# Residual rows of a graph layer's second stage loaded through GpSimd's queue instead of ScalarE's

## The chip, the cores and the metric

One core of a Trainium2 chip. The metric is the device time of one execution in microseconds (us), median of several runs. For the kernel before it is 1530.25 us over 3 runs (1523.82 to 1533.23).

## What is computed

x has 8 batches of 4096 nodes with 256 features, adj is 4096 x 4096, W is 256 x 256; all are 32-bit floats.

```python
HW = einsum('bnf,fo->bno', x, W)
A = relu((adj + adj.T) * 0.5)
D = sum(A, axis=1)
d = where(D > 0, D ** -0.5, 0)
L = eye(4096) - d[:, None] * A * d[None, :]
x = layernorm(x + relu(einsum('nm,bmo->bno', L, HW)), axis=-1, eps=1e-5)
```

The inputs make adj sparse: node j is linked to node i with a probability that falls with both indices, and the diagonal is always set.

## The kernel before

The nodes are cut into 32 rows of 128 nodes. One "row" of x, of the product or of the output is a tile of 128 partitions (nodes) by 2048 values (8 batches of 256), 1 MB.

**First stage** (lines 398 to 670). adj is read in blocks of 512 x 512, transposed on TensorE and added to its mirror block on VectorE, put through relu on ScalarE and stored to a scratch array in HBM, `a_dram`. On the way sums over groups of 64 columns are kept (`part`). HW, scaled by d, is formed row by row and stored as `g_dram` (4096 rows of 8 KB). The product of the first row of 128 output nodes (`lead`) is made here too, because all of its blocks are needed.

**Second stage** (lines 768 to 1051). It makes the other 31 output rows, in blocks u of two rows (2u+1 and 2u+2; the last block, 15, has one), in the order 1 to 7, 0, 8 to 15. Since A is sparse, only some nodes m matter for a block. Lists made on the fly from `part` by VectorE and TensorE (functions `prepare` and `lists`, lines 937 to 985) pack up to 128 such nodes into one tile of the list. A tile of the list serves one or both of the rows and 64 or 128 nodes of each; its kind says which. For each tile:

- GpSimd gathers the tile's pieces of A (`ga`, line 814, 128 x 128 or 128 x 256) and the 128 rows of g (`g`, line 827, 1 MB) with two indirect DMAs, in `gather(n)`. The g tiles go into a ring of RING = 12 buffers, so gather n + 12 is emitted behind the products of tile n.
- TensorE multiplies them into four PSUM banks per row (line 1032). The first row of a block uses the banks b0, the second the banks b1. Two products that fill 64 partitions each run side by side.

A block has 9 to 26 tiles (table CAPS). When a row's last product is emitted, `finish(i)` follows (line 907): ScalarE evicts the four banks through relu with the scale -d into one buffer y (line 683; there is one such buffer), then VectorE adds y to the residual row of x, `xr` (line 693), takes mean and variance (lines 702 to 721) and normalises in place (line 726), and SyncE's queue stores the result (line 734). The last row, 31, is finished in four parts spread over ScalarE, VectorE and GpSimd (`finish_last`, line 858; the adds are at lines 874, 876, 882 and 887).

**Residual rows.** The tiles `xr` come from a pool of four 1 MB buffers (`blocks_pool`, line 395; shared with the first stage's blocks of adj). `residual(i, engine)` takes a buffer and issues one DMA on the queue of the engine given (line 677); in HBM the row is 1024 pieces of 1 KB. A buffer is free when the store of the row four places back has landed. Row 0's and the first block's are loaded by SyncE's queue ahead of the stage.

**Order of the work.** The program is written down in one order, and each engine takes its instructions in that order. `queue(engine)` pins an instruction behind the instruction last emitted on that engine, so that the scheduler does not move it. `after(n, fn, ...)` puts a piece of work off until n units of products are emitted; a unit is a tile's product for 64 nodes of one row. At the start of each block, `residuals` is put off by 10 units (4 for the last block):

```python
if new:
    after(6, prepare, u)
    if q > 0:
        after(10 if u != SEQ[-1] else 4, residuals, range(2 * u + 1, 2 * u + 1 + blocks(u)))
```

So the pair of residual loads of a block stands, in the emitted order, some five to ten tiles into the block. On ScalarE the neighbours of the pair are the evictions of the block before and those of the block itself; on GpSimd the neighbours are the gathers that run 12 tiles ahead of the products.

Of the kernel before, what the change touches and what calls it, by code (L numbers as in the profile page):

```python
# [59 lines left out]
def kernel(  # L60
# [25 lines left out]
    nc = tc.nc  # L86
# [88 lines left out]
    def blocks(u):  # L175

        return min(2, NB - 1 - 2 * u)
# [497 lines left out]
    def residual(i, engine):  # L675
        xr = blocks_pool.tile([P, B, F], F32, tag="adj", name=f"xr_{i}")
        engine.dma_start(xr, x[:, i * P : (i + 1) * P, :].rearrange("b p f -> p b f"))
        return xr
# [89 lines left out]
    with (  # L768
# [23 lines left out]
        def queue(engine):  # L792

            traced = reversed(nc.cur_bb.bb.instructions)
            return tc.issue_after(next(i for i in traced if i.engine == engines[engine]))
# [55 lines left out]
        xr = {i: residual(i, nc.sync) for i in (0, *range(2 * u + 1, 2 * u + 1 + blocks(u)))}  # L851
# [76 lines left out]

        def residuals(rows):
            for i in rows:  # L930
                with queue("act"):
                    xr[i] = residual(i, nc.scalar)


        ahead = {u: {k: SEQ[n + k] for k in (2, 3, 4) if n + k < NU} for n, u in enumerate(SEQ)}
# [58 lines left out]
        for q, (u, step) in enumerate(steps):  # L994
            new = q == 0 or steps[q - 1][0] != u
            last = q + 1 == len(steps) or steps[q + 1][0] != u
# [4 lines that stand above are left out]
                left = {}  # L1001
                for v, st in steps[q:]:
                    if v == u:
                        for k, t in st:
                            for b, _ in targets(u, k):
                                left[b] = left.get(b, 0) + 1
                begun = set()
                for b in range(blocks(u)):
                    py[2 * u + 1 + b] = []
# [103 lines left out]
```

## Time and profile before

| | us |
|---|---|
| median of 3 runs | 1530.25 |
| lowest and highest run | 1523.82, 1533.23 |
| profiled execution, span from the first to the last instruction | 1527.5 |
| PE busy | 1441.2 (94%) |
| DVE busy | 983.6 (64%) |
| POOL busy | 682.0 (45%) |
| ACT busy | 369.0 (24%) |
| L827, gathers of g, 268 | 294.9 busy |
| L814, gathers of A, 268 | 292.0 busy |
| L693, add of the residual, 31 | 71.1 busy |
| L677, residual loads on ScalarE's queue, 29 | 0.374 each to issue |

The page gives no time of the profiled execution other than its span; the runs' times are those of other executions.

PE is TensorE's matmul, PEld its weight loads, DVE is VectorE, ACT ScalarE, POOL GpSimd, SP SyncE. A number such as L827 is a line of the kernel. In the page's row pictures the span is cut into 40 slices of 38 us, and each digit is the busy share of a slice in tenths. The DMA row is the mean busy share of the core's 16 DMA engines. Matmuls are pipelined and their ends are modelled, so a full PE row alone does not say that PE is at its peak. In the lists of waits a line reads: engine, what waited, what it waited for, us in total, times, longest. Lines of the timeline read: start, length, engine, line, operation, out<-in, count, and in brackets the idle time before and what ended it.

### The profile page before, as it was taken

What the parts mean: (1) busy time and instruction counts of PE and PEld (TensorE: products, weight loads), DVE (VectorE), ACT (ScalarE), POOL (GpSimd) and SP (SyncE); (2) the same over time, 40 slices, a digit from 0 to 9 for tenths busy, and PEclk for the clock granted to TensorE, in tenths of its full rate; (3) what the DMA queues carried; (4) which work ended last, traced back from release to release, by engine and by line L of the source; (5) the groups of instructions that cost most, each with busy time, mean ns of one, the idle gap of its engine ahead of it and who ended that gap; (6) DMA issues with size and microseconds to landing.
All of it is one profiled execution on the core that took longest, in us unless ns stands there. A gap on an engine that the chain in (4) does not pass through costs nothing.

```text
span 1527.5 us, 19332 instructions
## 1 busy us (share of the span) xinstructions
PE 1441.2 (94%) x6440; PEld 763.6 (50%) x6440; DVE 983.6 (64%) x3015; ACT 369.0 (24%) x462; POOL 682.0 (45%) x1051
## 2 busy tenths in 40 slices
PE   5999999989989989999999999999999999999995
PEld 5778777767767754433343343333433433333331
DVE  4676578888646463055568769569137688898534
ACT  3655554535434450010100100100010010001111
POOL 3002010010303316666667666666556676656653
PEclk9999999989999999999999999999999999999998
DMA  9999999999879898999999999999979999999995
GB/s 340 365 366 401 393 379 365 359 369 354 344 248 367 332 390 354 401 395 418 361 393 372 402 409 365 393 403 389 384 278 406 346 394 403 405 393 366 379 405 195
DMA packets 216714, 564.50 MB, mean 370 GB/s; under 512 B 16550, under 2 KB 104918, under 8 KB 180134
## 3 DMA queue, kind: packets, MB, share of 16 engines
q0 software_dynamic: 54224, 304.94, 50.4%
q1 hardware_dynamic: 93472, 126.89, 23.8%
q10 hardware_dynamic: 68912, 131.37, 22.7%
q8 instruction: 54, 0.88, 0.2%
q14 instruction: 52, 0.43, 0.1%
HBM read 443.61 MB, written 136.34 MB: 380 GB/s over the span
## 4 chain that ended last, share of the span: by engine, by line
PE 68%; DMA 14%; DVE 9%; issue 5%; POOL 2%; ACT 2%; ACTq 0%; DVEq 0%; POOLq 0%
PE py L1032 49%; PE pg L532 8%; DMA g<-g_dram,gi 6%; PE lead L490 5%; DMA a_dram<-sym 5%; DVE sym L427 3%; PE xtr L521 2%; PE tr L423 2%; DVE part L432 2%; DMA xin<-in_x_dram 2%; DMA ga<-a_dram,ai 1%; ACT sym L431 1%; PE lists L356 1%; ACT xt L522 1%; POOL g L827 0%
## 5 line engine op out<-in xcount | busy, mean ns | idle before, releaser
L1032 PE MATMUL py<-g,ga 128*64 128x512 f32 (+1 forms) x2872 | 813.0, 600 | 18.4 <-DMA g<-g_dram,gi 8.0
L1032 PEld LDWEIGHTS py<-g,ga 128*64 128x64 f32 (+1 forms) x2872 | 293.1, 151 | 525.1 <-issue 493.1
L827 POOL DMA_INDIRECT g<-g_dram,gi x268 | 294.9, 1101 | 219.1 <-PE py L1032 79.1
L814 POOL DMA_INDIRECT ga<-a_dram,ai x268 | 292.0, 1090 | 109.5 <-issue 76.8
L683 ACT ACTIVATE y<-py,minus_r 128x512 f32<-128x512 f32 x120 | 79.9, 687 | 812.3 <-PE py L1032 659.8
L693 DVE TENSOR_TENSOR xr<-xr,y 128x2048 f32<-128x2048 f32 x31 | 71.1, 2294 | 269.1 <-ACT y L683 267.2
L532 PE MATMUL pg<-w_sb,xt 128*128 128x256 f32 x1024 | 232.0, 385 | 5.2 <-ACT xt L522 5.2
L427 DVE TENSOR_TENSOR sym<-tr,adj 128x512 f32<-128x512 f32 x256 | 162.7, 683 | 96.9 <-PE tr L423 80.2
L532 PEld LDWEIGHTS pg<-w_sb,xt 128*128 128x128 f32 x1024 | 195.6, 194 | 33.4 <-ACT xt L522 5.6
L432 DVE TENSOR_REDUCE part<-sym 128x32 f32<-128x2048 f32 x64 | 145.5, 2279 | 62.0 <-ACT sym L431 62.0
L423 PE MATMUL tr<-ident,adj 128*128 128x128 f32 x1024 | 138.4, 285 | 30.6 <-DVE sym L427 19.2
L431 ACT ACTIVATE sym<-sym 128x2048 f32<-128x2048 f32 x64 | 122.6, 1916 | 129.9 <-DVE sym L427 117.5
L452 POOL TENSOR_TENSOR r<-e,neg_half 128x4 f32<-128x4 f32 x8 | 8.3, 1039 | 317.9 <-DVE e L451 236.5
L423 PEld LDWEIGHTS tr<-ident,adj 128*128 128x128 f32 x1024 | 118.6, 146 | 60.4 <-DVE sym L427 32.1
L521 PE MATMUL xtr<-ident,xin 128*128 128x128 f32 x512 | 72.4, 288 | 18.0 <-DVE sym L427 16.5
L702 DVE BATCH_NORM_STATS2 stats<-xr 128x6 f32<-128x256 f32 x256 | 87.0, 413 | 1.1
L726 DVE TENSOR_SCALAR xr<-xr,mv,root 128x256 f32<-128x256 f32 x248 | 83.6, 409 | 0.1
L490 PE MATMUL lead<-gt,strip 128*128 128x512 f32 x176 | 83.0, 598 | 0.0
L522 ACT COPY xt<-xtr 128x512 f32<-128x512 f32 x128 | 68.1, 591 | 46.7 <-PE xtr L521 46.0
L542 ACT ACTIVATE gt<-pg,r 128x512 f32<-128x512 f32 x88 | 60.6, 688 | 74.8 <-PE pg L532 72.3
L1032 PE MATMUL py<-g_hub,ga 128*128 128x512 f32 x176 | 77.3, 592 | 0.0
L521 PEld LDWEIGHTS xtr<-ident,xin 128*128 128x128 f32 x512 | 59.0, 146 | 34.9 <-DVE sym L427 26.4
(142 smaller groups left out, 825.8 us busy)
## 6 DMA issues: line engine op xcount, KB each, us to landing
adj<-in_adj_dram SPq DMA_DIRECT2D x64, 1024.0 KB
a_dram<-sym ACTq DMA_DIRECT2D x64, 1024.0 KB
out_dram<-xr SPq DMA_DIRECT2D x31, 1024.0 KB
xr<-in_x_dram ACTq DMA_DIRECT2D x29, 1024.0 KB
xin<-in_x_dram SPq DMA_DIRECT2D x44, 512.0 KB
g_dram<-gt ACTq DMA_DIRECT2D x22, 1024.0 KB
xin<-in_x_dram POOLq DMA_DIRECT2D x20, 512.0 KB
g_dram<-held ACTq DMA_DIRECT2D x10, 1024.0 KB
```

The lines of the kernel that those rows point to most:

```text
L423: ins = nc.tensor.transpose(pt[:, c * P : (c + 1) * P], tji[:, c, a * P : (a + 1) * P], ident)
L427: nc.vector.tensor_add(sym[:, a, :], pt, tij[:, a, :])
L431: nc.scalar.activation(sym, sym, AF.Relu, scale=0.5)
L432: nc.vector.tensor_reduce(part[:, i * A : (i + 1) * A, j * S // Q : (j + 1) * S // Q], sym.rearrange("p a (c q) -> p a c q", q=Q), AX.X, A ...
L490: nc.tensor.matmul(lead[c], lhsT=strip, rhs=g[:, c * S : (c + 1) * S], start=not done, stop=len(done) == NB - 1, skip_group_check=True,)
L521: nc.tensor.transpose(pt[:, k, c, :], xin[b // H][:, b % H + k, c * P : (c + 1) * P], ident)
L532: ins = nc.tensor.matmul(pg[:, k * FO : (k + 1) * FO], lhsT=xt[:, b + k, c, :], rhs=w_sb[:, c, :], start=(c == 0), stop=(c == FC - 1),)
L702: nc.vector.bn_stats(stats[:, b, :], z[:, b, :])
L726: nc.vector.tensor_scalar(z[:, b, :], z[:, b, :], mv[:, b, 0:1], rstd[:, b : b + 1], ALU.subtract, ALU.mult,)
L814: nc.gpsimd.indirect_dma_start(out=at if both else at[:, :P], out_offset=None, in_=a_pairs if both else a_rows, in_offset=bass.IndirectOff ...
L827: nc.gpsimd.indirect_dma_start(out=gt, out_offset=None, in_=g_dram, in_offset=bass.IndirectOffsetOnAxis(ap=gi[:, t : t + 1], axis=0), boun ...
L1032: nc.tensor.matmul(py[2 * u + 1 + b][c][rows, :], lhsT=at[:, off + rows.start : off + rows.stop], rhs=gt[:, c * S : (c + 1) * S], start=ne ...
```

## The change

The function that issues the residual loads of a block names another engine, both for the DMA and for the pin on the order. The point in the emitted order stays.

```diff
         def residuals(rows):
             for i in rows:
-                with queue("act"):
-                    xr[i] = residual(i, nc.scalar)
+                with queue("pool"):
+                    xr[i] = residual(i, nc.gpsimd)
```

It concerns 29 loads of 1 MB: the rows of all blocks but the first. In the built program the instructions of TensorE, VectorE and SyncE keep their order. ScalarE loses 29 DMA issues. GpSimd gains 29, in pairs between two pairs of gathers, and the last one behind the last gather.

## Prediction

> **What bounds the kernel now.** I read the page first: busy shares, the 40 slices, the DMA queues.
>
> ```profile
> PE   5999999989989989999999999999999999999995
> POOL 3002010010303316666667666666556676656653
> DMA  9999999999879898999999999999979999999995
> ```
>
> From slice 16 on (about 600 us, the second stage) TensorE and the DMA engines are both full, and GpSimd is half busy. The stretch view puts numbers on it; its columns are the stretch, its length, busy time and instruction count of PE, PEld, DVE, ACT and POOL, then the granted clock, the DMA share and GB/s.
>
> ```profile
> 595.00:1150.00 555.00, 545.06 (x2109) 208.78 (x2109) 331.38 (x1267) 42.78 (x65) 364.86 (x339) 0.99 0.99 383
> 1150.00:1507.00 357.00, 348.71 (x1416) 131.21 (x1414) 265.22 (x1004) 37.82 (x56) 220.52 (x201) 0.99 1.00 386
> ```
>
> PE is busy for 893.8 of 912 us, so about 18 us is all that any better supply of data can give before the last products. The weight loads agree: they follow each other every 0.43 us, and the pauses over 1.1 us from start to start add up to 19 us, of which 5.6 lie between 1450 and 1500 us. The waits of GpSimd say what paces the gathers:
>
> ```profile
> POOL g L827 <- PE py L1032: 79.1, 56, 4.6
> POOL g L827 <- DMA g<-g_dram,gi: 48.6, 40, 2.8
> POOL ga L814 <- DMA g<-g_dram,gi: 24.9, 28, 2.0
> ```
>
> A gather waits for PE to free a ring buffer, or for an earlier gather's landing: in the built program every GpSimd DMA waits for the one eight places before it, so eight (four pairs ga and g) are in flight. The chain of waits shows that as steps of 13.0 to 14.2 us "DMA g" between 1436 and 1507 us. Matching each gather with the product that uses it, it is issued 13 to 40 us ahead of its use. The tightest are 12.6 us (near 921), 17.2 (1428) and 13.6 (1486).
>
> Now the residual loads. ScalarE issues them in pairs right after the last eviction of the block before, and VectorE's add needs them:
>
> ```profile
> 1441.98 3.93 ACTq L677 DMA_DIRECT2D xr<-in_x_dram  x2
> 1487.29 0.37 ACTq L677 DMA_DIRECT2D xr<-in_x_dram  x1
> ```
>
> ```profile
> 1430.32 2.29 DVE L693 TENSOR_TENSOR xr<-xr,y 128x2048 f32<-128x2048 f32 x1 [15.32 <-ACT y L683]
> 1442.64 2.29 DVE L693 TENSOR_TENSOR xr<-xr,y 128x2048 f32<-128x2048 f32 x1 [0.31 <-ACT y L683]
> 1476.44 2.29 DVE L693 TENSOR_TENSOR xr<-xr,y 128x2048 f32<-128x2048 f32 x1 [22.77 <-ACT y L683]
> 1489.28 2.29 DVE L693 TENSOR_TENSOR xr<-xr,y 128x2048 f32<-128x2048 f32 x1 [1.83 <-issue]
> ```
>
> The trace's packet records show the pair landing one behind the other, slowly: issued at 1442, landed at 1456.0 and 1488.5; issued at 678.5 and 679, landed at 693.3 and 718.6. The last one, issued at 1487.3, landed at 1510.9, and the first add that needs it starts at 1512.6.
>
> [...]a queue of 1 KB packets beside one of 4 to 8 KB packets gets a small share (26 to 75 GB/s against 250 to 365 for GpSimd's queue in the packet records).[...] The trace has 50 of 536 gathers above 1.5 us instead of 0.95 to 1.0, many of them starting within a microsecond of an L693 add.
>
> **The change part by part.** Removed from ScalarE's queue: 29 issues of 0.374 us. ScalarE idles 660 us before its evictions waiting for PE, so this gives nothing. Nor did the waits of these loads for their buffer: the longest hold it between 1345.9 and 1358.1, and its next eviction is at 1378.3.
>
> Added to GpSimd: 29 issues. No load of 1 MB in 1 KB runs is there on GpSimd, but its half is: xin took 758 ns for 512 runs, and 128 runs of 1 KB take 592 ns, so 1024 runs come to 758 + 512 x (758 - 592)/384 = 979 ns. Bounds: 758 ns, and twice 758 = 1516 ns. I take 1.0 us and 0.3 us between issues: 2 x 1.3 = 2.6 us per block of about 51 us. A pair of gathers needs 0.95 + 1.0 + 2 x 0.3 = 2.55 us, and pairs follow at 3.4 us (912/268), so some 15 pairs leave 12.7 us. Hidden; at 1516 ns it is 3.6 us, hidden too. If that cover were gone, 38 us would be at stake.
>
> Moved in time: a load now stands between the gathers of the same point in the emitted order. Counting GpSimd's DMAs, those points lie in the run before at 707, 772, 842, 904, 964, 1022, 1076, 1165, 1221, 1273, 1326, 1377, 1428 and 1475 us, and behind the very last gather (1497.7). That is 18 to 41 us later than now (10 for the last). In one queue with the gathers a load lands about 13 us after its issue, like a gather, and the second 3 us later. For the first load of each pair against its add:
> - 720 (add at 734.8), 785 (797.6), 1178 (1187), 1234 (1238.6), 1286 (1288): in time.
> - 855 (854.7), 1339 (1338.0): level.
> - 917 (911.4), 977 (970.8), 1035 (1029.6), 1390 (1384.1): 6 us late.
> - 1441 (1430.3), 1488 (1476.4): 11 to 12 us late.
>
> The second loads are all earlier than now or in time. What is late next where an add is 6 to 12 us late? Behind it on VectorE stand the statistics, the index lists and the add of the second row. The lists are first used by a gather 18 us or more after they are made (1439.2 to 1465.7, 1297.9 to 1318.4), so that holds. The second row's eviction needs the y buffer that the add frees: at 1441 + 2.3 = 1443.3 against 1439.4 now, but PE's next block writes the first row's banks for 3.4 us before it needs the second's; at 1490.3 against 1484.7 the last block uses the other banks alone. I cost it at nothing, up to 4 us. The wait for the buffer (the store four rows back) is over at least 10.8 us before each point (1261.6 against 1272.4 is the narrowest).
>
> Gathers behind a pair: 2.1 MB at 386 GB/s is 5.5 us of queue in front of them. But the same bytes no longer compete before that point, so the gathers before it run ahead; the count of bytes at the end of a block is equal. Nothing, up to 5.5 us where the lead is 12.6 to 17.2 us.
>
> DMA time itself. Three lines of the DMA view from 640 to 1500 us (packets, MB, share of 16 engines), and for GpSimd's loads the line of 347 to 531 us, where it moved xin in 1 KB runs:
>
> ```profile
> q0 software_dynamic: 45904, 269.62, 78.8%
> q10 hardware_dynamic: 30043, 30.30, 10.4%
> q1 hardware_dynamic: 29937, 30.19, 10.0%
> ```
>
> ```profile
> q0 software_dynamic: 3600, 11.73, 17.3%
> ```
>
> ScalarE's queue (q10) costs 0.104 x 860/30.30 = 2.95 us per MB, GpSimd's with 1 KB runs 0.173 x 184/11.73 = 2.71. A load gets 0.24 x 1.05 = 0.25 us cheaper, 29 of them 7.3 us. It counts only where PE then waits: the ring is nearly full (mostly 10 or 11 of 12 out) until 1310 us, so the 7 loads after it count, 7 x 0.25 = 1.8 us.
>
> The end. Between 1475 and 1507 us PE waits for gathers (2.9 and 1.8 us shown at 1500 and 1507). The last row's load, some 0.9 MB of which now moves before the last gather lands, then stands behind it: 0.9/0.386 = 2.4 us earlier. It lands about 3 us after that gather, and the products and evictions ahead of its add take 5.5 us. VectorE must do two rows of 11.0 us (1476.4 to 1487.5) after the late load: 1488 + 22.2 = 1510, against the 1513.4 at which the last row's add starts; a 4.2 us gain is just kept.
>
> Sum against the profiled execution: 1527.5 - 1.8 - 2.4 = 1523.3 us of span. The median of the runs, 1530.25, is 2.75 above that span (the page gives no other time of that execution), so 1526.0.
>
> **The rivals.** (1) Hidden anyway: PE paces everything, the freed DMA time is not used: 1530. For it: PE busy 98%; against it: the waits at the end.
> (2) Slower, gathers queue behind the bursts: where the lead is under 13 + 5.5 us a pair costs up to 5.5 us that PE doesn't regain. Places: 842, 904 to 921, 1428, 1475 to 1486, some three to four blocks, 16 to 22 us: 1547. It decides from three full losses on. For it: leads of 12.6 and 13.6; against it: bytes conserved.
> (3) Slower, late residuals hold VectorE: it is without a pause before its adds at 1238.6 and nearly so at 1288 and 1338. If loads land 10 us later than I say[...], each of four blocks loses about 8 us: 1562. It decides once a load is over 7 us late there, the lead of the lists' inputs (1233.8 against 1240.1).
> (4) All of the DMA saving counts, and the stores of rows 29 and 30 also slip behind the last gather (1 MB, 2.7 us): 1530.25 - 7.3 - 2.4 - 2.7 = 1518.
>
> **How the numbers follow.** Forecast 45%, (1) 23%, (2) 17%, (3) 6%, (4) 9%. A measurement here tells about 1% from no change (the three runs lie 0.6% apart). Faster by over 1% (under 1515): half of (4), 0.05. Slower by over 1% (over 1545.5): (3) and most of (2), 0.20. The rest, 0.75, is within 1%. The likeliest case alone runs from 1519 to 1532; the range that leaves out a tenth at either end is 1515 to 1549.
>
> **What would show it.** Right: L677 on GpSimd at about 1 us each; DMA share still 0.99 to 1.00; first loads landing 13 us after issue, adds at the four late points waiting for xr, the second adds earlier; PE's pauses after 1450 shorter; last gather landing a few us sooner. Wrong: new PE waits for g right behind the residual loads;[...] PE waiting for lists.

## The result, and the profile after

| | median us (lowest to highest) | runs |
|---|---|---|
| before | 1528.05 (1523.23 to 1533.23) | 17 |
| change | 1534.93 (1530.02 to 1538.35) | 17 |

The ratio is 1.0041 with the interval 1.0029 to 1.0053: the change is slower by 0.4%, some 6 us. The forecast was 1526.0, 4.2 us faster than the 1530.25 that three runs of the kernel before had given; over 17 runs that kernel's median is 2.2 us lower. The time lies in the range of 1515 to 1549, but it moved the other way. A repetition (e4 below) gave 1.0036.

The profiled execution of the change has a span of 1533.0 us. Its first add of the second stage starts at 601.5 us, against 595.7 before and 597.3 to 598.7 in four other profiles (e1 to e4 below, the change itself once more among them). Those 6 us are chance in a stage that the change does not touch. So times of the two profiles are compared here with 5.8 us taken off, and the net effect is read from the medians, not from the two spans.

The page of the kernel after, same rows as shown of before:

```profile
PE   5999998989989989999999999997999999999996
POOL 3002000010202225776667776776657687676663
DMA  9999999999879999999999999999979999999996
```

The stretches of the second stage (length; busy time and count of PE, PEld, DVE, ACT, POOL; granted clock, DMA share, GB/s):

```profile
595.00:1150.00 555.00, 540.26 (x2078) 207.21 (x2078) 325.32 (x1223) 43.09 (x64) 379.93 (x349) 0.99 0.98 381
1150.00:1507.00 357.00, 350.83 (x1438) 132.66 (x1436) 267.70 (x1011) 40.08 (x60) 248.96 (x224) 1.00 1.00 386
```

GpSimd's digits are up by one (once by two) in half of the slices: 15.1 + 28.4 = 43.5 us more in these stretches, of which the 29 issues are some 27. The DMA engines are about as full as they were (share 0.98 and 1.00, before 0.99 and 1.00). PE is busy for less of the first stretch (540.3 for 545.1 us) and for more of the second (350.8 for 348.7); with the stretches moved by 5.8 us its two numbers are the same. The groups of the residual tile (duration in ns: minimum, median, maximum; first and last start):

```profile
L693 DVE TENSOR_TENSOR xr<-xr,y x31: 2277/2292/2333, 601.5 to 1505.1; 128x2048 f32<-128x2048 f32 x31
L677 POOL DMA_DIRECT2D xr<-in_x_dram x29: 902/949/971, 710.9 to 1503.8; - x29
```

GpSimd's waits in the kernel after:

```profile
POOL g L827 <- PE py L1032: 62.9, 47, 5.9
POOL g L827 <- DMA g<-g_dram,gi: 19.9, 23, 1.3
POOL ga L814 <- DMA xr<-in_x_dram: 9.7, 6, 2.5
POOL g L827 <- DMA xr<-in_x_dram: 7.8, 5, 2.8
POOL xr L677 <- DMA g<-g_dram,gi: 2.2, 3, 1.0
```

A residual load issues in 0.95 us and hardly waits itself. Gathers now wait for residual loads among the eight places, 17.5 us in 11 waits, but they wait less for each other. What is new stands in PE's waits in the second stage. Before, PE waited mainly for gathered g, and once for VectorE's `pos_k`:

```profile
PE py L1032 <- DMA g<-g_dram,gi: 8.0, 5, 2.9
PE py L1032 <- issue: 6.9, 13, 0.8
PE py L1032 <- DVE pos_k L188: 2.2, 1, 2.2
```

After:

```profile
PE py L1032 <- DVE pos_k L188: 10.6, 2, 8.2
PE py L1032 <- issue: 4.1, 3, 1.9
PE py L1032 <- DVE half L720: 4.1, 1, 4.1
PE py L1032 <- DMA g<-g_dram,gi: 1.8, 3, 1.2
```

The longest of the waits with "issue" after, 1.92 us at 1359.5, ends 0.06 us behind an L188, at the end of the same block as the 2.2 us before (1349.4). So that one is not new.

Products do not read `pos_k`. It is the place on VectorE's queue behind which something came free, and the timeline of one block shows what. The first fence is the kernel before, the second the kernel after, at the end of the same block (lines picked from the timeline):

```profile
1029.62 2.29 DVE L693 TENSOR_TENSOR xr<-xr,y 128x2048 f32<-128x2048 f32 x1 [8.07 <-ACT y L683]
...
1032.94 0.96 PE L356 MATMUL lists<-val,hot 128*128 128x30 bf16 x32
...
1033.82 14.58 PE L1032 MATMUL py<-g,ga 128*64 128x512 f32 x57
...
1037.75 0.17 DVE L368 COPY low<-lists 128x15 f32<-128x15 f32 x1
...
1040.26 0.52 DVE L188 TENSOR_TENSOR pos_k<-incl_k,lists 128x352 f32<-128x352 f32 x1
```

```profile
1028.00 1.87 POOL L677 DMA_DIRECT2D xr<-in_x_dram  x2
...
1032.80 0.95 PE L356 MATMUL lists<-val,hot 128*128 128x30 bf16 x32
...
1033.68 8.80 PE L1032 MATMUL py<-g,ga 128*64 128x512 f32 x40
...
1039.49 2.29 DVE L693 TENSOR_TENSOR xr<-xr,y 128x2048 f32<-128x2048 f32 x1 [7.87 <-issue]
...
1041.88 2.42 ACT L683 ACTIVATE y<-py,minus_r 128x512 f32<-128x512 f32 x4 [13.02 <-DVE xr L693]
...
1047.86 0.17 DVE L368 COPY low<-lists 128x15 f32<-128x15 f32 x1
...
1050.14 0.52 DVE L188 TENSOR_TENSOR pos_k<-incl_k,lists 128x352 f32<-128x352 f32 x1
...
1050.72 5.72 PE L1032 MATMUL py<-g,ga 128*64 128x512 f32 x11 [8.24 <-DVE pos_k L188]
```

The two PSUM tiles of `lists(u)` carry the tag b0: they take two of the four banks that the first row of the next block accumulates in. They are free when VectorE has read them (L368 to L189; the first of the two behind L188), and VectorE does that behind the first row's add, its statistics and its inverse root, 8.1 us of work. Before, the add starts at 1029.6, L188 is done at 1040.8 and L189 at 1041.3, and PE does not stop. After, the load issued at 1028.0 lands 11.5 us later, the add starts at 1039.5, L188 at 1050.1, and PE, done with its 40 products at 1042.5, stands 8.24 us. The word "issue" in the bracket of L693 says only that the profile shows no releaser. That it is the load follows from the order: y had been evicted before, and in e3 below the same wait has the load named. The late add also keeps the second row's eviction (L683) 13.02 us from the one buffer y, but that eviction is over at 1044.3, more than 6 us before PE resumes.

That two banks are what PE waits for is read from the program and from the releaser that the trace names (PE resumes 0.06 us behind L188); no run put the lists into other banks.

In block 13 there is no L188 any more, and the last reading of the lists is L369:

```profile
1448.16 2.29 DVE L693 TENSOR_TENSOR xr<-xr,y 128x2048 f32<-128x2048 f32 x1 [22.15 <-issue]
...
1450.55 2.42 ACT L683 ACTIVATE y<-py,minus_r 128x512 f32<-128x512 f32 x4 [11.81 <-DVE xr L693]
...
1456.62 0.17 DVE L369 SCALAR_TENSOR_TENSOR low<-lists,low 128x9 f32<-128x9 f32 x1
...
1456.93 4.11 PE L1032 MATMUL py<-g,ga 128*64 128x512 f32 x8 [4.06 <-DVE half L720]
```

Here too the eviction of the second row stands for y, 11.81 us. But that eviction is over at 1453.0, and PE resumes only at 1456.93, 0.14 us behind the end of L369. The bracket names L720, which stands a few instructions ahead of L369 on VectorE; the second profile of the change names L369 itself at this place. So this pause too is put down to the lists' banks.

PE's pauses of 1 us or more add up to 19.3 us in the second stage of this execution, against 9.3 before.

### The profile page after: what moved, and what is told of

The parts are those of the page before. It is cut to its first block, busy times and chain, and to the rows that moved or that the text cites. A ratio compares the mean times of both kernels' runs of the same rounds, so it can differ in the third digit from the quotient of the medians.

```text
span 1533.0 us, 19317 instructions
## 1 busy us (share of the span) xinstructions
PE 1442.1 (94%) x6440; PEld 767.6 (50%) x6440; DVE 988.2 (64%) x3015; ACT 370.0 (24%) x462; POOL 721.8 (47%) x1080
## 2 busy tenths in 40 slices
DMA packets 194442, 564.50 MB, mean 368 GB/s; under 512 B 16550, under 2 KB 75222, under 8 KB 157862
## 4 chain that ended last, share of the span: by engine, by line
PE 51%; DMA 16%; issue 15%; DVE 11%; POOL 5%; ACT 1%; ACTq 0%; another core or an unknown queue 0%; POOLq 0%; DVEq 0%; SPq 0%
PE py L1032 34%; DMA g<-g_dram,gi 7%; PE pg L532 7%; PE lead L490 5%; DMA xr<-in_x_dram 3%; DVE sym L427 2%; DMA ga<-a_dram,ai 2%; PE tr L423 2%; PE xtr L521 2%; DVE part L432 2%; DMA a_dram<-sym 2%; DMA xin<-in_x_dram 2%; POOL g L827 2%; POOL ga L814 1%; DMA adj<-in_adj_dram 1%
## 5 line engine op out<-in xcount | busy, mean ns | idle before, releaser
L1032 PE MATMUL py<-g,ga 128*64 128x512 f32 (+1 forms) x2872 | 809.3, 598 | 20.9 <-DVE pos_k L188 10.6
L827 POOL DMA_INDIRECT g<-g_dram,gi x268 | 301.7, 1126 | 181.5 <-issue 70.7
L814 POOL DMA_INDIRECT ga<-a_dram,ai x268 | 296.9, 1108 | 106.0 <-issue 81.0
L683 ACT ACTIVATE y<-py,minus_r 128x512 f32<-128x512 f32 x120 | 80.4, 687 | 820.4 <-PE py L1032 668.3
L693 DVE TENSOR_TENSOR xr<-xr,y 128x2048 f32<-128x2048 f32 x31 | 71.0, 2291 | 267.3 <-ACT y L683 175.0
L532 PE MATMUL pg<-w_sb,xt 128*128 128x256 f32 x1024 | 235.1, 388 | 5.2 <-ACT xt L522 5.2
```

What stands on the lines that cost most here:

```text
L532: ins = nc.tensor.matmul(pg[:, k * FO : (k + 1) * FO], lhsT=xt[:, b + k, c, :], rhs=w_sb[:, c, :], start=(c == 0), stop=(c == FC - 1),)
L814: nc.gpsimd.indirect_dma_start(out=at if both else at[:, :P], out_offset=None, in_=a_pairs if both else a_rows, in_offset=bass.IndirectOff ...
L827: nc.gpsimd.indirect_dma_start(out=gt, out_offset=None, in_=g_dram, in_offset=bass.IndirectOffsetOnAxis(ap=gi[:, t : t + 1], axis=0), boun ...
L1032: nc.tensor.matmul(py[2 * u + 1 + b][c][rows, :], lhsT=at[:, off + rows.start : off + rows.stop], rhs=gt[:, c * S : (c + 1) * S], start=ne ...
```

## The experiments

The theory, called "late" here: a first row's residual that comes late makes VectorE wait ahead of the add, the read-out of the lists behind it comes late, and PE waits for their two banks. Its rivals: GpSimd's own time for the 29 issues delays the gathers; the 2 MB bursts in the gathers' queue delay them (the prediction's second rival). Ratios are to the kernel before on the same chip, with a 95% interval; medians are in us. A ratio can differ from the quotient of the two medians by about 0.1%. The fillers of e6 to e10 work on a spare tile that nothing reads; no kernel leaves out any part of the computation.

**e4, the change once more.** No edit; the yardstick for e1 to e3, which ran beside it.

> The change once more, for a second profile. Theory late: again pauses of PE of 4 to 9 us ending with VectorE's read-out of the lists or with ScalarE's eviction, at ends of blocks whose first residual is late. A theory that the loss sits in the first stage (its code is the same; in the profile of the change it ran 5.8 us longer): the first product of the second stage starts near 600 us again instead of 595. If that is chance, it starts anywhere from 594 to 601. 6 us above the kernel before.

1529.8 against 1524.19, ratio 1.0036 [1.0023, 1.0050]. In its profile PE waits for the read-out of the lists longer than in the first one:

```profile
PE py L1032 <- DVE pos_k L188: 17.7, 4, 8.8
PE py L1032 <- DVE low L369: 3.7, 1, 3.7
```

**e1, first rows back on ScalarE's queue, second rows on GpSimd's.**

```diff
-                with queue("pool"):
-                    xr[i] = residual(i, nc.gpsimd)
+                with queue("act" if i % 2 else "pool"):
+                    xr[i] = residual(i, nc.scalar if i % 2 else nc.gpsimd)
```

> First rows of each pair stay on ScalarE's queue, second rows go through GpSimd's. Theory late (the first row's residual lands after its product is evicted, VectorE stands before its add, and the list read-outs and the y buffer behind that add hold TensorE): the first rows are early again, so no pause of PE over 3 us with a VectorE releaser; 0 to 6 us under the kernel before, 8 to 12 under the change. Theory burst (gathers queue behind the 2 MB in GpSimd's queue): half the burst stays, so half of the loss, 3 us above the kernel before. Theory issue (GpSimd's own time at the issues): 15 of 29 issues stay, 3 us above the kernel before.

1521.84, ratio 0.9991 [0.9977, 1.0005]. PE's waits are those of before in kind:

```profile
PE py L1032 <- DMA g<-g_dram,gi: 14.2, 8, 2.6
PE py L1032 <- DVE pos_k L188: 1.9, 1, 1.9
```

The loss comes with the loads of the first rows, the ones that were late. This leaves open whether it helped that GpSimd has half as many issues.

**e2, both loads on GpSimd, asked for 5 units earlier. e11, 5 units later.**

```diff
-                    after(10 if u != SEQ[-1] else 4, residuals, range(2 * u + 1, 2 * u + 1 + blocks(u)))
+                    after(5 if u != SEQ[-1] else 4, residuals, range(2 * u + 1, 2 * u + 1 + blocks(u)))
```

> All on GpSimd's queue as in the change, but the pair put off by 5 units instead of 10, so about 8.6 us earlier. Theory late: the adds that were 6 to 12 us late are on time or at most 3 us late, 0 to 5 us under the kernel before; if the buffer is not free yet GpSimd stands at L677 for a few us. Theories burst and issue: same queue, same bytes, same issues, so as the change, 6 us above the kernel before.

> All on GpSimd's queue as in the change, put off by 15 units instead of 10, so 8.6 us later still. Theory late: the first adds come 8 to 20 us late in most blocks and the pauses of PE grow with them, 20 to 50 us above the kernel before. Theories burst and issue: same bytes, same issues, as the change, 6 us above the kernel before.

With 5 units: 1525.32 against 1524.19, 1.0009 [0.9998, 1.0021]. With 15: 1548.07 against 1532.40, 1.0114 [1.0078, 1.0149]. With the change's 10 it was 1.0036 to 1.0041. Issues, queue and bytes are the same in all three; the place in the order differs, with it the lateness and the gathers that stand behind a pair, and the time follows it. (The 15.7 us at 15 units are less than the 20 to 50 that "late" forecast.) PE's wait for the lists in the profiles goes the same way: 5.3 us at 5 units, 10.6 and 17.7 at 10, and at 15 (PE's waits in e11):

```profile
PE py L1032 <- DVE pos_k L188: 24.4, 5, 9.1
```

**e3, the change, with the lists read ahead of the first row's add.** The add and what follows it are put off until the read-out has been emitted.

```diff
-            after(1, rest)
+            if i % 2:
+                put_off[i] = rest
+            else:
+                after(1, rest)
...
                         in_turn(run, steps)
+                elif 2 * u + 1 in put_off:
+                    put_off.pop(2 * u + 1)()
```

> As the change, but VectorE reads the lists out of PSUM before it adds the first row's residual. Theory late: the pauses of PE that end with the list read-out (8.2 us at 1043 in the profile of the change) go, those in which the eviction waits for the y buffer stay or grow by the 3 us of the read-out; 0 to 3 us above the kernel before. Theories burst and issue: 6 us above the kernel before, as the change.

1521.23, ratio 0.9988 [0.9976, 1.0001]; against e4 beside it that is 8.6 us less by the medians, 7.3 by the ratios. The same block in its timeline:

```profile
1020.86 0.93 POOL L677 DMA_DIRECT2D xr<-in_x_dram  x1
...
1026.46 0.95 PE L356 MATMUL lists<-val,hot 128*128 128x30 bf16 x32
...
1029.82 0.52 DVE L188 TENSOR_TENSOR pos_k<-incl_k,lists 128x352 f32<-128x352 f32 x1
...
1034.94 2.29 DVE L693 TENSOR_TENSOR xr<-xr,y 128x2048 f32<-128x2048 f32 x1 [4.04 <-DMA xr<-in_x_dram]
...
1037.32 2.42 ACT L683 ACTIVATE y<-py,minus_r 128x512 f32<-128x512 f32 x4 [14.80 <-DVE xr L693]
...
1040.71 11.74 PE L1038 MATMUL py<-g,ga 128*128 128x512 f32 x34 [2.84 <-DMA g<-g_dram,gi]
```

The first row's load still lands only 14.1 us after its issue and the add still waits 4.0 us for it, but the lists are read at once, and PE waits for nothing but g (15.9 us in 9 waits over the stage). All 29 issues and all bursts are still in GpSimd's queue. So neither of them makes the loss; the order on VectorE does. The run also settles the y buffer: evictions stand for it longer than in the change (14.80 us here, 111.8 us in 10 waits over the stage), and no wait of PE's products ends with one of them.

**e5, the kernel before with the lists first. e12, e1 with the lists first.** Is reading the lists first a gain by itself, which would make e3 say less?

> The kernel before (residuals on ScalarE's queue) with the list read-out ahead of the first row's add. It tells whether the 8.6 us that the same edit brought to the change are the edit's own or undo the change's loss. Theory late: in the kernel before the adds are hardly late and one pause of 2 us is all that ends with the read-out, so 0 to 2 us under the kernel before. If the edit is simply good for any version: 6 to 9 us under it.

> Both mends together: first rows on ScalarE's queue, second rows on GpSimd's, lists read out ahead of the add. Theory late: nothing of the loss is left, 2 to 6 us under the kernel before, no better than each mend alone by more than 2 us. Theory burst: half of the loss stays, 3 us above the kernel before.

e5: 1531.72 against 1531.54, 1.0007 [0.9992, 1.0023]. e12: 1530.60 against 1532.40, 0.9992 [0.9978, 1.0006]. Neither shows a gain. The edit has a price that could hide one: PE waited for VectorE's `kind` (L216) ahead of the lists' own matmuls, 11.7 us in e5 and 13.4 us in e12, 3 waits each, which e3 has not. But PE's wait for that reading is 2.2 us in the profile before, and a gain from reading sooner should not be much more than that; this is argued, not measured. By it, most of what lies between e4 and e3 is the lateness taken away. The pauses of e5 add up to 22.5 us, against 9.3 in the profile before, and yet its median is the same: a sum of pauses is not a cost. Gathers that run ahead while PE stands may give time back later; no run shows how much.

**e6 and e10, GpSimd's time alone.** The kernel before, with two adds of 128 x 256 on GpSimd per residual load (0.62 us each alone), about the time of an issue; no transfer moves.

```diff
+        spare = lpool.tile([P, F], F32, name="spare")
+        nc.gpsimd.memset(spare, 0.0)
...
                     xr[i] = residual(i, nc.scalar)
+                for _ in range(2):
+                    with queue("pool"):
+                        nc.gpsimd.tensor_add(spare, spare, spare)
```

> The kernel before, with two adds of 128 x 256 on GpSimd (about 1.3 us) at each of the 29 places where the change issues a residual load; a filler on data that nothing uses. Theory issue: GpSimd's time at these places is what costs, so 4 to 6 us above the kernel before. Theory late: the ring covers it, within 1 us of the kernel before.

> GpSimd's filler at the 29 places again, without the set-up on GpSimd that held the first gathers of the stage for 10 us (a pause of PE at 607 us that belongs to that run's own edit). Theory issue: 6 to 10 us above the kernel before. Theory late: within 2 us of it.

e6: 1551.43, 1.0121 [1.0100, 1.0142], and it missed its aim: the memset that clears the tile waited 20.3 us on GpSimd for the first stage, ahead of the first gathers, and PE stood 10.35 us at 607. e10 clears the tile on VectorE: 1539.74 against 1532.40, 1.0037 [1.0019, 1.0055]. So GpSimd's time is not free, which I had not expected of an engine that is half busy. In blocks 5 to 7 it is behind; one such place of e10 (GpSimd alone):

```profile
1026.27 2.69 POOL L937 TENSOR_TENSOR spare<-spare 128x256 f32<-128x256 f32 x4
1029.11 3.03 POOL L816 DMA_INDIRECT ga<-a_dram,ai  x1
1032.45 1.01 POOL L829 DMA_INDIRECT g<-g_dram,gi  x1 [0.30 <-issue]
```

From there it issues back to back to 1047. Taken alone, e10 speaks for GpSimd's time as the cause: it costs as much as the change, "late" had allowed it 2 us, and 7.3 us by the medians is what "issue" had forecast. But e3 keeps the 29 real issues and does not lose, and PE's long pauses after the change name the lists, while those of e10 do not: there PE has 13.1 us in 21 short waits with no releaser named (6.9 in 13 before) and the same single 2.2 us for `pos_k`. The filler is also longer than what it stands for: four adds take 2.69 us, a pair of issues 1.87. Whether that is why the adds cost and the issues do not was not tried.

**e7, e8 and e9, VectorE held without any transfer moved.** The kernel before, with 20 adds of 128 x 256 on VectorE (0.43 us each, some 9 us) in blocks 5, 6, 7, 13 and 14, at three places: ahead of the first row's add (e7), behind the read-out of the lists (e8), between the add and the statistics (e9).

```diff
+        def hold():
+            for _ in range(20):
+                with queue("dve"):
+                    nc.vector.tensor_add(spare, spare, spare)
```

> The kernel before, residuals on ScalarE's queue and early, with some 7 us of filler on VectorE ahead of the first row's add in blocks 5, 6, 7, 13 and 14, those where the change's add came late. Theory late: PE pauses of 3 to 9 us return at the ends of these blocks, ending with the list read-out or the eviction; 5 to 9 us above the kernel before, with no transfer moved. Theories burst and issue: VectorE has slack there, within 1 us of the kernel before.

> The same filler in the same blocks, but behind the list read-out. Theory late: what matters is what stands ahead of the read-out, so at most 2 us above the kernel before. If VectorE's time as such is what is short there: as with the filler ahead, 5 to 9 us above.

> The kernel before, residuals on ScalarE's queue and early, with the same 8.5 us of filler on VectorE in blocks 5, 6, 7, 13 and 14, now between the first row's add and its statistics: the list read-out comes 8.5 us later, the y buffer is freed as before, no transfer is moved. (The filler ahead of the add ran in the time in which VectorE waited for the eviction, 908.8 to 917 us, and so held nothing up.) Theory late: PE pauses ending with the list read-out return, 4 to 9 us at block 7, 2 to 4 at 5 and 6; with the eviction free of it none at 13 and 14 or less than in the change; 4 to 8 us slower than the kernel with the filler behind the read-out. Theories burst and issue: equal to that kernel within 2 us.

e7: 1530.74 against 1531.54, 0.9993 [0.9979, 1.0007]. It missed its aim: the adds ran in the time in which VectorE had been waiting for the eviction. In block 5 they ended at 918.0, 1.9 us behind the eviction; in the other four blocks they ended ahead of it and held up nothing. e8: 1526.16, 0.9967 [0.9950, 0.9984], a little faster. e9: 1549.30 against 1532.40, 1.0114 [1.0080, 1.0148]. Timeline of e9 in the block shown above:

```profile
1034.89 9.16 DVE L912 TENSOR_TENSOR spare<-spare 128x256 f32<-128x256 f32 x20
...
1036.59 0.96 PE L356 MATMUL lists<-val,hot 128*128 128x30 bf16 x32
...
1052.28 0.52 DVE L188 TENSOR_TENSOR pos_k<-incl_k,lists 128x352 f32<-128x352 f32 x1
...
1052.85 3.34 PE L1046 MATMUL py<-g,ga 128*64 128x512 f32 x8 [6.57 <-DVE pos_k L188]
```

Here the residuals come through ScalarE's queue in time, the add is not late and y is free as before. Only the statistics and the lists behind them are some 9 us later, and PE's pauses are of the change's kind: 7.3, 7.4 and 6.6 us for `pos_k` in blocks 5 to 7 and 3.6 us for L369 in block 13. The same filler behind the read-out costs nothing. That shows the mechanism apart from queue, bytes and GpSimd. The loss is larger than the change's, and than the 4 to 8 us over e8 that "late" had forecast, since here the lists are 9 us late in all three blocks.

**A version that beats both?** Of the versions of the change e1 and e3 come nearest, at 0.9991 and 0.9988 with intervals that reach past 1. Against the change both win about half a per cent; against the kernel before, neither is shown to win.

## Why the prediction was wrong, point by point

- **What bounds the kernel: right.** PE (891.1 of 912 us busy in the two stretches after) and the DMA engines (share 0.98 and 1.00) are full, and the change's cost shows in PE's pauses (19.3 us for 9.3).
- **29 issues on GpSimd: right in size.** 0.95 us measured for the estimated 1.0. "Hidden" holds for these issues (e3), with less room than I gave it (e10).
- **Where the loads land, and which adds are late: right.** I named 855, 1339 as level and 917, 977, 1035, 1390, 1441, 1488 as late by 6 to 12 us. In the profile after, the first adds that wait with "issue" are those at 860.0, 920.3, 980.1, 1039.5, 1395.3, 1448.2 and 1493.5. Less the 5.8 us of the first stage, the first is level with before, the next four stand 3 to 5 us behind those of before, and the last two 11 to 12.
- **"What is late next ... I cost it at nothing, up to 4 us": this step failed.** It asked when a gather first uses the lists, found 18 us of room, and wrote "so that holds". But the lists have an earlier deadline: until VectorE has read them they hold two of the banks b0, and the next block's products want those about 9 us after the lists are made (1033.7 to 1042.5 in the block shown). Before, L188 was done at 1040.8, so the room was about 2 us, not 18. The kernel before shows it too: its one PE wait for `pos_k`, 2.2 us at 1349, is this very edge. What it costs: 14.7 us of PE pauses for VectorE in one profile of the change and 21.4 in the other, against 2.2 before; in the medians some 6 us.
- **The y buffer, at nothing: right as far as PE shows.** In block 13 the eviction began at 1450.55, with 5.8 taken off 5.4 us later than before, where the step had put 4; but it was over before the lists let PE go on, and in e3 longer waits for y hold no product.
- **Gathers behind a burst, nothing to 5.5 us: nothing.** Gathers waited 17.5 us for residual loads, but PE's wait for g went from 8.0 to 1.8 us. I put that down in part to PE, which, held elsewhere, let the gathers run ahead; in e3, which shows no wait of PE but for g, it is 15.9 us. The second rival, slower by 16 us through the bursts, is refuted by e3 all the same.
- **DMA time, 7.3 us cheaper: mis-sized.** The DMA view of the kernel after, 640 to 1500 us:

```profile
q0 software_dynamic: 53409, 299.21, 88.7%
q1 hardware_dynamic: 29249, 29.48, 9.7%
```

  GpSimd's queue carries 29.59 MB more than before for 9.9 points more of 860 us: 2.88 us per MB, against 2.95 on ScalarE's queue. I had taken 2.71 from the first stage. That saves 0.07 us per MB, some 2 us for all 29 loads, of which the last few count: half a microsecond for the 1.8 us in the sum.
- **The end, 2.4 us: seen, but not kept.** Before, PE paused 2.91 and 1.79 us for g at 1500 and 1507. After, it runs on:

```profile
1494.52 24.53 PE L1032 MATMUL py<-g,ga 128*64 128x512 f32 x104
```

  In these two profiles that gives back most of what the blocks lost: the last row's first eviction, at 1516.5, is with 5.8 us taken off 1 us earlier than the 1511.9 of before. Since e1, which loses nothing in the blocks, has such pauses at the end again (2.2, 1.9 and 2.5 us), the end goes by the gathers' supply in these profiles: the late PE of the change found its data there. So it is mostly a refund of the loss, not a gain of the change. By the medians the refund is not complete. The sum for the end had two slips besides: 0.9/0.386 is 2.3, and a VectorE that is free at 1510.2 leaves a gain of 3.2 us ahead of 1513.4, so 4.2 would not have been "just kept".
- **The third rival, late residuals that hold VectorE: nearest to the truth, with the wrong place.** I looked for it in the blocks in which VectorE has no pause before its adds (1239, 1288, 1338), and for loads 10 us later than I said; those 10 us were my supposition, and no trace had shown them. It came in the blocks where VectorE has idle time, with loads as late as I said, through the order behind the add.

What stays open: why e8 is 0.3% faster than before, and why GpSimd's filler costs 0.4%. The two profiles of the change differ in which blocks pause, so a sum over pauses does not give the 6 us exactly.

## What to carry to other kernels

When an instruction will wait longer, go through everything queued behind it on its engine and list for each piece not only who reads its result, but which buffers and PSUM banks stay taken until it has run, and who wants those next. Put the short work that frees a bank ahead of the instruction that waits for a transfer: here that took 8.6 us off by the medians (e3 against e4). When a load changes queues, keep its lead over its first use, not its place in the program: here 5 units earlier brought back nearly the whole loss (1.0009 for 1.0036).

## What the runs showed of the hardware

**After some short pauses PE ran at half its clock.** Before, the pauses of 2.37 us (to 933.5), 2.17 (to 1349.4) and 2.91 (to 1500.1) are each followed by about 3.4 us at half the clock (granted 0.50; 1.00 on either side); so is one of 1.50 us after (to 697.3). In the spell at 934 the products, two of 64 partitions side by side, start a pair every 0.77 to 0.91 us, behind it (to 937.7) every 0.43. So the four pairs that start in it take some 1.7 us longer, on top of the pause. Others of 1.79 us (before, 1507.1), 1.92 and 2.34 us (after, 1359.5 and 991.1) are not followed by such a spell. One more before, at 988.0, follows no pause over 1 us but four of 0.77 us within 6 us. In the 8.24 us pause and behind it the clock was halved for 10.2 us, 5 of them after PE had resumed. Stretches around it in the kernel after (the third column from the end is the clock):

```profile
1000.00:1050.00 50.00, 42.48 (x176) 16.43 (x173) 35.48 (x126) 5.17 (x8) 35.50 (x32) 0.95 1.02 402
1050.00:1100.00 50.00, 49.28 (x128) 19.74 (x129) 33.25 (x125) 0.00 (x0) 33.61 (x32) 0.95 0.99 380
```

In the clock records the spells named are 3.41 us long, the one at the 8.24 us pause 10.24 us. What decides between the pauses that bring a spell and those that do not, no run here settles.

**1 KB rows cost the DMA engines about the same on either queue** (640 to 1500 us): 2.88 us per MB on GpSimd's, 2.95 on ScalarE's, although GpSimd's queue moved them in fewer, larger packets (194442 packets in the execution instead of 216714, for the same 564.50 MB).

**Gathers beside a long TENSOR_TENSOR of VectorE were often slow to issue.** In the profile before, 45 of the 89 gathers that overlap one of over 1 us (by 0.05 us or more) take more than 1.5 us to issue instead of 0.95 to 1.0; of the 447 others 5 do. The change left the number of slow ones about as it was, 50 before and 54 after.
